# Four constants on SyncE's queue, and other planned times in the first sequence of a Flamingo kernel

## The chip, the cores and the metric

The kernel runs on one core of a Trainium2 chip. The metric is the time of one execution on the device, in microseconds (us). The kernel before was timed three times; its profile is of one further execution.

## The reference

Input `x` is 8 sequences of 256 tokens with 512 channels, `ctx` has the same shape. Two layers follow each other, each of an attention-like recurrence (`wkv`) and a feed-forward part, each added to `x` with a gate tanh(g):

```python
x = x + tanh(g_xattn[0]) * wkv0(layernorm(x), ctx)       # decay w, bonus u; a scan over 256 tokens
x = x + tanh(g_ffn[0])   * ffn0(layernorm(x))            # 512 -> 2048 -> 512
x = x + tanh(g_xattn[1]) * wkv1(layernorm(x), ctx)
x = x + tanh(g_ffn[1])   * moe1(layernorm(x))            # 8 experts, 2 for each token
# wkv: k = layernorm(x), v = ctx, one step of the scan for each token and channel
#   y_t = (e1 * p + e2 * v_t) / (e1 * q + e2);  p, q = running sums with decay w, kept stable by a running maximum o
# ffn0: hidden = silu(x W1^T) * (x W3^T); hidden = fwht(hidden) / sqrt(2048); out = hidden W2^T
# moe1: route by x gate^T, then silu(x w1) * (x w3), times w2, weighted by the route
```

`fwht` is a Walsh-Hadamard transform over the 2048 hidden units. The kernel applies it to W2 instead of to the hidden units: once with a 128 x 128 Hadamard matrix (`hadm`), once, after a turn of the rows through HBM, with a 16 x 16 one (`had16`).

## The kernel before, in words

Channels lie on partitions: a sequence's `x`, `ctx` and normed tiles are 128 partitions x 4 channel groups x 256 tokens, all in float32. Sequence 0 is taken in two halves of 128 tokens (b = 0, 1), so that TensorE gets its first large products earlier; sequences 1 to 7 are taken whole. In front of the loop over the sequences stand the loads and the first sequence:

- SyncE's queue loads x and ctx of sequence 0 by halves (`load_first`, L261 and L262), then W2 in 16 loads (L325) and W1 and W3 of the first feed-forward part in 16 (`fill_w13`, L279), then x of sequence 1 (`load_x`, L249). The transformed W2 is stored to `turned` (L631) and read back (`fill_w2`, L287) on the same queue.
- ScalarE's queue loads the constants with `load_const` (L301): `w0c`, `u0c`, `hadm`, `tgx` (gates of the recurrence), and then those that only later steps read: `w1c` and `u1c` (decay and bonus of layer 1), `tgf` (gates of the feed-forward parts) and `gate` (the router's weights). A DMA is started by an instruction in the engine's own stream, so what follows it on the engine waits for it.
- Each DMA waits, in the built program, for the landing of the DMA eight before it on the two queues together, as they share eight semaphores.

The steps that matter here, with their lines:

- `layernorm` (L434 to L473): VectorE adds the four channel groups (`s_k` or `s_f`, L434 and L436), TensorE takes the mean (`mean_k`, `mean_f`, L440), VectorE subtracts it (L442), ScalarE squares (`sq`, L446), VectorE adds (`q_k`, `q_f`, L450 and L452), TensorE takes the variance (`var`, L459), VectorE adds the epsilon (L464), GpSimd takes the power (L466), TensorE spreads it over the partitions (`rstd`, L471) and VectorE multiplies (L473). Names with `k` are norms ahead of a recurrence, names with `f` those ahead of a feed-forward part.
- `decayed_max`, the recurrence of layer 0, for each pair of channel groups: VectorE scans the running maximum (L545) and subtracts it (`dd`, L550), ScalarE makes the exponents (Relu, L557 and L559, then Exp, L562), VectorE adds the bonus to `dd` (L566) and multiplies by ctx (`ev`, L569), ScalarE takes `dd`'s Exp (L571), VectorE scans `q` (L574) and `p` (L576) and adds the denominator (L584). The three `carry` copies for the second half of the tokens are ScalarE's (L580). `attend` takes the reciprocal (L515), the products and the update of `x` (L509 to L521).
- `transform` (L623 and L625): one matmul of a 128 x 512 block of W2 with a Hadamard matrix into one of three PSUM banks `ps_o`, and ScalarE's copy back into the weights. A float32 matmul of the program is two MATMUL rows in the trace. `fwht_kj` is the first pass of 16 transforms and their stores, and runs as three lines in parallel; `fwht_i` is the second pass.
- `set_up` prepares the constants of later steps on ScalarE and VectorE (L391 to L412): `w1c` becomes the decay of layer 1, `tgf` gets its tanh, `had16` is made from `hadm`.
- `unit` (L798 to L809) is one hidden unit block of the feed-forward part: 8 matmuls into a PSUM bank `gl` (three banks), tanh on ScalarE (`t_f`, L805), two products on VectorE (L807, L809).

The order in which the instructions stand on TensorE, ScalarE, VectorE and GpSimd is not left to the compiler. While it is built, the kernel keeps a plan: each step is a `Line`, a generator that names an engine and a planned length before it writes its instructions (`pe`, `dve`, `act`, `pool`), and a line that is due at the earliest planned time is written next. `until` gives a step an earliest planned time; `near[0]` is the planned gap between two steps of one line on the same engine, `least[0]` the shortest planned matmul. For the first sequence (`alone(0, 1)`) the plan has its own values, and after it the ordinary ones. The planned times have no effect on the chip other than through this order: each engine works through its own stream in order and waits where a semaphore tells it to.

Behind the first sequence each sequence s runs its hidden units and its output on TensorE, with the recurrence of s + 1 (layer 0) and of s - 1 (layer 1) worked in beside it, and then the tokens are sent to the queues of their experts. Experts 6 and 7 are begun early, and the eight experts' products fill the rest of the time from about 770 us.

Of the kernel before, what the change touches and what calls it, by code (L numbers as in the profile page):

```python
# [17 lines left out]
P = 128  # L18
# [5 lines left out]
DC = D // P  # L24
# [5 lines left out]
NE = 8  # L30
# [20 lines left out]
def flamingo_kernel(  # L51
# [20 lines left out]
    nc = tc.nc  # L72
# [10 lines left out]
    def v4(name, shape=(P, DC, T)):  # L83
        return work.tile(list(shape), FP, tag="v4", name=name, bufs=35)
# [34 lines left out]
    lines = []  # L119
    LATER = 1e9  # L120
    near = [0.16]
    least = [0.28]
    SLACK = 0.8
    WAIT = 0.25
# [5 lines left out]
        return "V", 0.09 + 0.00105 * slope * width, False  # L130

    def act(width, slope=1.0):
        return "A", 0.2 + 0.0008 * slope * width, False

    POWER = ("G", 0.8, False)

# [7 lines left out]
    def until(time):  # L144
        return "T", time, False
# [54 lines left out]
    def joined(n, make):  # L200
        ends = []

        def told(at):
            ends.append(at)
            if len(ends) == n:
                make(max(ends))

        return told
# [14 lines left out]
    def alone(*levels):  # L223
        while any(line.level in levels for line in lines):
            start, i = min((line.starts(), i) for i, line in enumerate(lines))
            next(
                line for line in lines if line.op[0] == lines[i].op[0] and line.starts() <= start + WAIT
            ).write()
# [11 lines left out]
    queue = dram.tile([NE * NT, ROW], FP, name="queue")  # L240
# [6 lines left out]
    def load_x(s):  # L247
        x[s] = v4(f"x{s}")
        nc.sync.dma_start(out=x[s], in_=x_in[:, :, s * T : (s + 1) * T])  # L249
# [9 lines left out]
    def load_first(b):  # L259
        bs = slice(b * P, (b + 1) * P)  # L260
        nc.sync.dma_start(out=x[0][:, :, bs], in_=x_in[:, :, bs])  # L261
        nc.sync.dma_start(out=first_ctx[:, :, bs], in_=ctx_in[:, :, bs])  # L262
# [4 lines left out]
    def new_w13(name):  # L267
        return tuple(
            [[v4(f"{t}_{name}_{i}{j}", (P, 2, D)) for j in range(2)] for i in range(2)] for t in ("w1", "w3")
        )  # L270
# [4 lines left out]
    def fill_w13(tiles, *srcs):  # L275
        for j in range(2):
            for t, src in zip(tiles, srcs):
                for i in range(2):
                    nc.sync.dma_start(  # L279
                        out=t[i][j],  # L280
                        in_=src[i * 2 * P : (i + 1) * 2 * P, j * D : (j + 1) * D].rearrange("(c p) h -> p c h", p=P),
                    )
        return tiles
# [12 lines left out]
    def w2_of(w, k):  # L296
        return w[k // 2][:, k % 2, :]

    def load_const(src, shape, name):
        t = const.tile(shape, FP, tag=name, name=name)  # L300
        nc.scalar.dma_start(out=t, in_=src)  # L301
        return t

    load_first(0)
    w0c, u0c = load_const(w0, [P, DC], "w0c"), load_const(u0, [P, DC], "u0c")

    early = const.tile([P, 1], FP, tag="early", name="early")
    nc.vector.memset(early, 0.0)
    nc.scalar.activation(early, early, AF.Square)
    hadm = load_const(had, [P, P], "hadm")  # L310
    tgx = load_const(g_xattn.partition_broadcast(P), [P, 2], "tgx")
    load_first(1)
    wcol = [w0c, load_const(td1, [P, DC], "w1c")]
    ucol = [u0c, load_const(tf1, [P, DC], "u1c")]
    tgf = load_const(g_ffn.partition_broadcast(P), [P, 2], "tgf")
    gate = load_const(gateT, [P, DC, NE], "gate")

    w2h = [new_w2(n) for n in "ab"]
    turned = dram.tile([H0, D], FP, name="turned")
# [1 line left out]
    def by_kj(ap, i):  # L321
        return ap.rearrange("(k j i) d -> i k j d", j=8, i=16)[i]

    for i in range(16):
        nc.sync.dma_start(out=w2_of(w2h[i // KC], i % KC), in_=by_kj(W2T, i))  # L325
    w13 = [fill_w13(new_w13(n), *(w[:, i * HH : (i + 1) * HH] for w in (W1T, W3T))) for i, n in enumerate("ab")]
    load_x(1)


    def constant(shape, name, dt=FP):  # L330
# [13 lines left out]
        out=before, in_=ones, compare_op=ALU.is_gt, fill=0.0, base=0,  # L344
# [39 lines left out]
    def set_up_x():  # L384
        yield act(2)
        nc.scalar.activation(tgx, tgx, AF.Tanh)

    def set_up():

        yield act(4)  # L390
        nc.scalar.activation(wcol[1], wcol[1], AF.Exp)  # L391
        yield act(2)
        nc.scalar.activation(tgf, tgf, AF.Tanh)
        yield dve(4)
        nc.vector.tensor_scalar(wcol[1], wcol[1], -1.0, None, ALU.mult)

        yield act(4)
        nc.scalar.activation(decay, wcol[1], AF.Exp)
        yield dve(4)
        nc.vector.tensor_scalar(less, ucol[1], -1.0, 0.0, ALU.mult, ALU.min)  # L400
        yield dve(4)
        nc.vector.tensor_scalar(more_u, ucol[1], 0.0, None, ALU.min)
        yield dve(1)
        nc.vector.tensor_scalar(tgf_half, tgf[:, 1:2], 0.5, None, ALU.mult)
        yield dve(16)
        nc.vector.tensor_copy(token, token_i)


        yield dve(P)
        nc.vector.tensor_tensor(had16, hadm, hadm[:, 112:113].to_broadcast([P, P]), ALU.mult)  # L410
        for base, sign in ((0, 1), (15, -1)):
            nc.gpsimd.affine_select(  # L412
                out=had16, in_=had16, compare_op=ALU.is_ge, fill=0.0, base=base,
                pattern=[[-16 * sign, 8], [0, 16]], channel_multiplier=sign,
            )
# [75 lines left out]
    def first_norm(b):  # L491
        bs = slice(b * P, (b + 1) * P)
        yield from layernorm(x[0][:, :, bs], first_k[:, :, bs], f"k0_0_{b}")
# [125 lines left out]
    def transform(mat, i, scale):  # L619
        yield pe(D)  # L620
        w = w2_of(w2h[i // KC], i % KC)
        ps = ps_o.tile([P, D], FP, tag="o", name=f"fw_{i}")
        nc.tensor.matmul(ps, lhsT=mat, rhs=w, start=True, stop=True)  # L623
        yield act(D)
        nc.scalar.activation(w, ps, AF.Copy, scale=scale)  # L625

    def fwht_kj(j):
        for i in range(j, 16, 3):
            yield until(12.0 + 0.8 * i)
            yield from transform(hadm, i, 1.0)  # L630
            nc.sync.dma_start(out=by_kj(turned, i), in_=w2_of(w2h[i // KC], i % KC))  # L631

# [2 lines left out]
    def fwht_i():  # L635
        for h in range(2):
            latest_load[0] = fill_w2(w2h[h], turned[h * HH : (h + 1) * HH, :])
        return [chain(*(transform(had16, k, 0.5 / H0 ** 0.5) for k in range(j, 16, 2))) for j in range(2)]
# [713 lines left out]
    norm = [first_norm(b) for b in range(NB)]  # L1352
# [8 lines left out]
        mybir.EngineType.PE, mybir.EngineType.Activation, mybir.EngineType.DVE, mybir.EngineType.Pool  # L1361
    }
    with tc.manual_schedule(engines=ordered):
        near[0], least[0] = 0.08, 0.5

        finals = [
            joined(2, lambda at, b=b: Line(norm_f[b], level=2 * b, at=at)) for b in range(NB)
        ]
        second = [
            joined(2, lambda at, hf=hf: Line(half[1][hf], level=2, at=at, then=(finals[1],))) for hf in range(2)  # L1370
        ]

        def first_halves(at):
            for hf in range(2):
                Line(half[0][hf], level=0, at=at, then=(finals[0], second[hf]))

        Line(norm[0], level=0, at=3.7, then=(first_halves,))
        Line(norm[1], level=2, at=22.0, then=second)
        Line(set_up_x(), level=1, at=7.0)
        Line(set_up(), level=2, at=45.0)  # L1380
        turns = [Line(fwht_kj(j), level=1, at=0.0) for j in range(3)]
        alone(0, 1)
        near[0], least[0] = 0.16, 0.28
    fw = fwht_i()
    take(clear_queues())
    with tc.manual_schedule(engines=ordered):
# [182 lines left out]
```

## Time and profile before

| | us |
|---|---|
| timed runs (3): median | 1506.26 |
| timed runs: lowest, highest | 1505.01, 1506.66 |
| profiled execution: its own time | 1504.14 |
| profiled execution: span from first to last instruction | 1502.4 |
| TensorE busy in the span | 1460.9 (97%) |
| mean granted TensorE clock | 0.992 |

In the profile's rows a time is counted from the start of the span. A row of the timeline has start, duration, engine, line of the kernel, operation, output and inputs, shape and count; in brackets stands how long the engine was idle before it, and what ended that. `SPq` and `ACTq` are the sequencers of SyncE and ScalarE, where DMAs are issued. A row with a count merges instructions that follow each other. In the answers by stretches of time the count beside a busy time is that of the instructions, and the granted clock is a share of full speed; no clock is on record before 17 us, where 1.00 is printed.

### The profile page before, as it was taken

Reading aid. Unit: us, or ns where it says so; the run is one execution under the profiler, and the core shown is the slowest. Engines: PE = TensorE matmul, PEld = TensorE weight load, DVE = VectorE, ACT = ScalarE, POOL = GpSimd, SP = SyncE. Lnnn points to the kernel's source line nnn. Section 1 sums busy time; section 2 is a strip of 40 time slices with the busy share of each in tenths; the row PEclk is TensorE's granted clock in tenths of the full one; section 3 lists DMA queues with packets and bytes.
Section 4 is the critical chain, followed back from the end, with each engine's and each line's share of the span. In section 5 each row is a group of like instructions: output and inputs, shape, how many; then the busy total and the mean of one; then the engine's idle time right before and its main releaser. Section 6 shows DMA issues by size and latency. Waiting matters only on the chain. (4 is left out here: it accounts for less than half of the span.)

```text
span 1502.4 us, 19409 instructions
## 1 busy us (share of the span) xinstructions
PE 1460.9 (97%) x7336; PEld 1243.9 (83%) x7336; DVE 981.1 (65%) x2288; ACT 288.4 (19%) x677; POOL 245.2 (16%) x258
## 2 busy tenths in 40 slices
PE   6999999999999999999999999999999999999996
PEld 3888888888888888888877667688988889898894
DVE  5772886968788697876538413476647666476763
ACT  4340313213032321312111200011101111111110
POOL 1110111212122121312112200112301011010110
PEclk9999999999999999999999999999999999999998
DMA  9970001001100110115061314165124151330110
GB/s 324 355 264 14 12 31 43 28 36 37 41 29 29 50 35 15 43 30 182 15 248 38 97 36 161 35 199 201 60 86 153 40 205 43 108 137 28 60 33 18
DMA packets 79498, 135.16 MB, mean 90 GB/s; under 512 B 13084, under 2 KB 26524, under 8 KB 79392
## 3 DMA queue, kind: packets, MB, share of 16 engines
q1 hardware_dynamic: 69280, 108.45, 21.1%
q0 software_dynamic: 8960, 25.25, 4.8%
q8 instruction: 62, 1.02, 0.3%
q14 instruction: 44, 0.36, 0.1%
q10 hardware_dynamic: 1152, 0.09, 0.1%
HBM read 100.05 MB, written 37.90 MB: 92 GB/s over the span
## 5 line engine op out<-in xcount | busy, mean ns | idle before, releaser
L798 PE MATMUL gl_f<-xn,w_a 128*128 128x256 f32 (+1 forms) x1152 | 234.5, 359 | 1.0 <-DVE xn L473 1.0
L798 PE MATMUL gl_f<-xn,w_b 128*128 128x256 f32 (+1 forms) x1152 | 226.2, 357 | 0.0
L798 PEld LDWEIGHTS gl_f<-xn,w_a 128*128 128x128 f32 x1152 | 200.4, 192 | 27.9 <-issue 4.5
L798 PEld LDWEIGHTS gl_f<-xn,w_b 128*128 128x128 f32 x1152 | 200.5, 192 | 23.1
L781 PE MATMUL gl<-q,w_e 128*128 128x256 f32 x768 | 173.4, 384 | 6.0 <-DVEq L1479 4.0
L781 PEld LDWEIGHTS gl<-q,w_e 128*128 128x128 f32 x768 | 146.1, 193 | 26.6 <-issue 7.2
L969 POOL DMA_INDIRECT out<-g,who_e x40 | 46.3, 1158 | 502.3 <-DVE g L1231 407.0
L870 PE MATMUL o_f<-t_f,w_b 128*128 128x256 f32 x512 | 118.7, 380 | 0.0
L870 PE MATMUL o_f<-t_f,w_a 128*128 128x256 f32 x512 | 117.3, 380 | 0.0
L870 PEld LDWEIGHTS o_f<-t_f,w_b 128*128 128x128 f32 x512 | 96.2, 190 | 12.5
L870 PEld LDWEIGHTS o_f<-t_f,w_a 128*128 128x128 f32 x512 | 96.2, 190 | 12.5
L805 ACT ACTIVATE t_f<-gl_f 128x256 f32<-128x256 f32 (+1 forms) x144 | 50.0, 358 | 286.5 <-PE gl_f L798 286.0
L807 DVE SCALAR_TENSOR_TENSOR t_f<-t_f,gl_f 128x256 f32<-128x256 f32 (+1 forms) x144 | 53.6, 380 | 72.8 <-ACT t_f L805 72.4
L1156 PE MATMUL pa<-q,w_e 128*128 128x168 f32 x384 | 62.6, 306 | 0.0
L798 PE MATMUL gl<-q,w_e 128*128 128x256 f32 x256 | 58.4, 380 | 0.7 <-ACT q L920 0.7
L1156 PEld LDWEIGHTS pa<-q,w_e 128*128 128x128 f32 x384 | 57.4, 190 | 1.8 <-issue 1.3
L798 PEld LDWEIGHTS gl<-q,w_e 128*128 128x128 f32 x256 | 48.0, 190 | 11.1 <-issue 4.3
L1147 PE MATMUL y<-w_e,h 128*80 128x512 f32 (+1 forms) x128 | 56.9, 592 | 0.0
L785 ACT ACTIVATE t<-gl 128x256 f32<-128x256 f32 x48 | 18.4, 384 | 190.5 <-PE gl L781 190.5
L961 POOL DMA_INDIRECT g<-out,who_e x40 | 44.8, 1121 | 60.9 <-DMA out<-g,who_e 30.3
L515 DVE RECIPROCAL e<-e 128x512 f32<-128x512 f32 (+1 forms) x18 | 53.8, 2990 | 0.1
L809 DVE TENSOR_TENSOR t_f<-t_f,gl_f 128x256 f32<-128x256 f32 (+1 forms) x144 | 53.4, 379 | 0.7
(259 smaller groups left out, 2267.3 us busy)
## 6 DMA issues: line engine op xcount, KB each, us to landing
w_e<-in_w1T SPq DMA_DIRECT2D x32, 512.0 KB
w_e<-in_w3T SPq DMA_DIRECT2D x32, 512.0 KB
w_e<-in_w2T SPq DMA_DIRECT2D x32, 512.0 KB
queue<-empty SPq DMA_DIRECT2D x8, 1290.0 KB
r<-queue SPq DMA_DIRECT2D x32, 256.0 KB
c<-in_ctxT SPq DMA_DIRECT2D x15, 512.0 KB
out<-xr SPq DMA_DIRECT2D x16, 256.0 KB
x<-in_xT SPq DMA_DIRECT2D x7, 512.0 KB
```

Source lines behind the costliest of these rows:

```text
L515: nc.vector.reciprocal(den, den)
L781: nc.tensor.matmul(ps, lhsT=w13_of(w, c, k), rhs=xn(c)[:, :width], start=(c == 0), stop=(c == DC - 1))
L785: nc.scalar.activation(t, gp, AF.Tanh, scale=0.5)
L798: nc.tensor.matmul(ps, lhsT=w13_of(w, c, k), rhs=xn(c)[:, :width], start=(c == 0), stop=(c == DC - 1))
L805: nc.scalar.activation(t, gp, AF.Tanh, scale=0.5)
L807: nc.vector.scalar_tensor_tensor(t, t, 1.0, gp, ALU.add, ALU.mult)
L809: nc.vector.tensor_tensor(t, t, lp, ALU.mult)
L870: nc.tensor.matmul(o, lhsT=w2_of(w2h[k // KC], k % KC)[:, c * P : (c + 1) * P], rhs=hs[k], start=(k == 0), stop=(k == 2 * KC - 1),)
L961: nc.gpsimd.indirect_dma_start(out=g, out_offset=None, in_=out[:end, :], in_offset=bass.IndirectOffsetOnAxis(ap=who[:, b : b + 1], axis=0) ...
L969: nc.gpsimd.indirect_dma_start(out=out[:end, :], out_offset=bass.IndirectOffsetOnAxis(ap=who[:, b : b + 1], axis=0), in_=g, in_offset=None ...
L1147: nc.tensor.matmul(ys[b][:rows, :], lhsT=ts[k][:, b * P : b * P + rows], rhs=w2_of(w2, k), start=(k == 0), stop=(k == KC - 1),)
L1156: nc.tensor.matmul(ps[:, to, :], lhsT=weights[:, c, k * P : (k + 1) * P], rhs=toks[:, c, :], start=(c == 0), stop=(c == 1),)
```

## The change

Three things are changed, all in the first sequence or ahead of it.

1. `load_const` takes a queue, and `w1c`, `u1c`, `tgf` and `gate` are loaded from SyncE's queue, behind the W2, W1 and W3 loads and ahead of x of sequence 1. Before, they were issued from ScalarE's queue behind `tgx`.
2. In the plan of the first sequence the fixed part of a ScalarE step (`base[0]`) is 0.1 us instead of 0.2, the gap `near[0]` is 0.0 instead of 0.08, and the first norm is planned from 3.2 us instead of 3.7. After the first sequence both values are what they were.
3. The 16 transforms of the first pass over W2 are planned 0.86 us apart instead of 0.8.

```diff
+    base = [0.2]
...
     def act(width, slope=1.0):
-        return "A", 0.2 + 0.0008 * slope * width, False
+        return "A", base[0] + 0.0008 * slope * width, False
...
-    def load_const(src, shape, name):
+    def load_const(src, shape, name, queue=nc.scalar):
         t = const.tile(shape, FP, tag=name, name=name)
-        nc.scalar.dma_start(out=t, in_=src)
+        queue.dma_start(out=t, in_=src)
         return t
...
     load_first(1)
-    wcol = [w0c, load_const(td1, [P, DC], "w1c")]
-    ucol = [u0c, load_const(tf1, [P, DC], "u1c")]
-    tgf = load_const(g_ffn.partition_broadcast(P), [P, 2], "tgf")
-    gate = load_const(gateT, [P, DC, NE], "gate")
...
     w13 = [fill_w13(new_w13(n), *(w[:, i * HH : (i + 1) * HH] for w in (W1T, W3T))) for i, n in enumerate("ab")]
+
+    wcol = [w0c, load_const(td1, [P, DC], "w1c", nc.sync)]
+    ucol = [u0c, load_const(tf1, [P, DC], "u1c", nc.sync)]
+    tgf = load_const(g_ffn.partition_broadcast(P), [P, 2], "tgf", nc.sync)
+    gate = load_const(gateT, [P, DC, NE], "gate", nc.sync)
     load_x(1)
...
         for i in range(j, 16, 3):
-            yield until(12.0 + 0.8 * i)
+            yield until(12.0 + 0.86 * i)
             yield from transform(hadm, i, 1.0)
...
-        near[0], least[0] = 0.08, 0.5
+        near[0], least[0], base[0] = 0.0, 0.5, 0.1
...
-        Line(norm[0], level=0, at=3.7, then=(first_halves,))
+        Line(norm[0], level=0, at=3.2, then=(first_halves,))
...
         alone(0, 1)
-        near[0], least[0] = 0.16, 0.28
+        near[0], least[0], base[0] = 0.16, 0.28, 0.2
```

## The prediction

> **What bounds the kernel now.** I read the page first, then the granted clock by stretches, then the timeline of the first 72 us, engine by engine.
>
> ```profile
> PE 1460.9 (97%) x7336; PEld 1243.9 (83%) x7336; DVE 981.1 (65%) x2288; ACT 288.4 (19%) x677; POOL 245.2 (16%) x258
> PE   6999999999999999999999999999999999999996
> ```
> TensorE is busy 97% of the span; the only poor slice that this change can reach is the first (0 to 37.6 us).
>
> ```profile
> 34.20:37.50 3.30, 3.30 (x18) 3.30 (x17) 0.00 (x0) 0.00 (x0) 0.00 (x0) 0.50 1.05 387
> 37.60:61.40 23.80, 21.82 (x193) 21.58 (x192) 20.70 (x60) 8.56 (x33) 4.45 (x6) 1.00 0.95 344
> 61.50:64.80 3.30, 3.14 (x15) 2.87 (x15) 1.92 (x7) 0.63 (x1) 0.71 (x1) 0.50 1.01 364
> 64.90:72.00 7.10, 6.32 (x54) 5.91 (x53) 6.25 (x21) 2.48 (x8) 0.86 (x1) 1.00 1.04 377
> 72.00:140.00 68.00, 68.00 (x411) 57.45 (x410) 32.52 (x69) 18.66 (x43) 5.61 (x5) 1.00 0.49 171
> ```
> Columns: stretch, length, busy PE, PEld, DVE, ACT, POOL, then granted clock. From 72 us TensorE never rests; before that there are two half-clock spells, each behind a pause. So what counts is when TensorE starts the second half of sequence 0 (70.64 below): whatever it starts earlier, the end comes earlier.
>
> ```profile
> 7.56 0.49 ACTq L301 DMA_DIRECT2D gate<-in_gateT  x1
> 8.10 0.63 ACT L446 ACTIVATE sq_k<-k 128x512 f32<-128x512 f32 x1 [4.86 <-DMA w1c<-in_td]
> 11.34 5.33 PE L623 MATMUL fw<-w_a,hadm 128*128 128x512 f32 x6
> 17.98 1.56 ACT L625 ACTIVATE w_a<-fw 128x512 f32<-128x512 f32 x3
> 18.62 4.56 PE L623 MATMUL fw<-w_a,hadm 128*128 128x512 f32 x10 [1.95 <-DMA w_b<-in_W2T]
> 23.01 5.31 PE L623 MATMUL fw<-w_b,hadm 128*128 128x512 f32 x12
> 28.16 0.38 PE L440 MATMUL mean_f<-s_f,mean_m 128*128 128x128 f32 x2
> 33.41 4.57 PE L798 MATMUL gl_f<-xn,w_a 128*128 128x128 f32 x24 [0.22 <-DVE xn L473]
> 45.52 0.69 DVE L434 TENSOR_TENSOR s_k<-x 128x512 f32<-128x512 f32 x1 [0.66 <-DMA x<-in_xT]
> 50.62 1.19 DVE L442 TENSOR_TENSOR k<-x,mean_k 128x1024 f32<-128x1024 f32 x1
> 60.26 0.58 PE L459 MATMUL var_k<-mean_m,q_k 128*128 128x1 f32 x4 [1.98 <-DVE q_k L452]
> 65.11 1.22 DVE L473 TENSOR_TENSOR k<-k,rstd_k 128x1024 f32<-128x1024 f32 x1 [0.25 <-PE rstd_k L471]
> 70.64 1.16 PE L798 MATMUL gl_f<-xn,w_a 128*128 128x128 f32 x8 [0.78 <-DVE xn L473]
> ```
> ScalarE's first real step stands behind the issue of `gate`, though its input ended at 6.49. Three W2 transforms fill the three `ps_o` banks and TensorE waits 1.95 us for ScalarE to empty one. Then 22 matmuls in a row, one each 0.429 us (10 in 18.62 to 23.01), carry it to `mean_f`: the queue, not `s_f` (ready at 26.6), sets 28.16. Later TensorE waits 1.98 us in its own order for sequence 1's `var_k`, and pays a half-clock spell after it.
>
> **The four constants.** They leave ScalarE's queue: `sq_k` starts at 6.49 + 0.06 = 6.55, 1.55 us earlier; the chain to `dd` moves with it. On SyncE they stand behind all first weights and ahead of x of sequence 1 and the `turned` stores: four issues of 0.33 to 0.49 us (the L301 rows), about 1.5 us, hidden because that queue waits on landings there (`x` issued at 33.89, landed at 45.5). The waits in the built program tie each load to the landing of the one eight before it; four tiny loads take four of those places, so `x` is issued about 5 us later but still behind the same bytes. `x` is now first read near 48.8. `w1c` is first used by ScalarE near 46.1, and VectorE's negation stands behind that near 47.0, ahead of the scan, the denominator and the reciprocal. Its landing: lower bound 42 (the five weight tiles ahead at 1.35 us a tile, the pace at which L279's last loads are issued), upper 46.5 (11.6 us, as for `x`, from an issue near 35). I take 43: no cost.
>
> **The plan's figures.** The shorter step (0.1 for 0.2 us), the gap (0.0 for 0.08), the start 3.2 and the spacing 0.86 add no instruction: the built program has the same instructions on TensorE, VectorE, ScalarE and GpSimd, less the four issues; only their order in the first 140 us differs. On GpSimd the two selects of `had16` move behind one half's products (done near 53, used near 68): nothing.
>
> **The transforms.** In the built order one copy-out (L625) comes ahead of the three `carry` copies, and `dd`'s Exp (L571) after all four Relus. ScalarE's chain from 13.54 to 17.71 is back to back, so by its own steps the first copy-out starts at 16.04 (was 17.98) and TensorE resumes at 16.04 + 0.63 = 16.67 (was 18.62). But `dd`'s Exp loses 0.3 of its 1.55.
> Starting at 9.79, the first three transforms run at 0.853 a matmul until the clock rises, then 0.429: done near 14.3, so the pause is 2.4 us. In the trace a 3.41-us stretch less than about 30% busy (30.7 to 34.1, where `gl_f` fills the last 0.73; 58.0 to 61.4) was followed by half clock, one 55% busy (17.1 to 20.5) was not. If the stretches lie as before, 13.7 to 17.1 is 27% busy: I take half clock from 17.1 to 20.5, 5 matmuls done by then, 17 x 0.429 = 7.3 left: `mean_f` at 27.8 (-0.4) and not 26.1 (-2.1).
> [...]
>
> **The norms of sequence 0 and 1.** `mean_f` to first `gl_f` is an unbroken chain of 5.25 us (28.16 to 33.41): 33.04. Half clock again from 34.15; `rstd_k` after 24 matmuls at 37.16 (was 37.82), VectorE's k at 37.47 (was 38.13, -0.66). Then VectorE is the bound. Start to start from the rows:
> - Ahead of half 0's reciprocal (52.68) there go the wait for `x` 0.66, the second add of `s_k` 0.34, `had` 0.20, k's subtraction 1.12 and a scan 0.61: 2.93. 52.68 - 0.66 - 2.93 = 49.1; one wait for a `t_f` makes it 49.3.
> - To half 1's reciprocal (58.10, 5.42 later) come `had` 0.20, scan 0.61, add 0.34, and `q_k` 0.60 goes: 55.3.
> - To `s_f` (61.08, 2.98 later) comes k's 1.12, and 0.48 goes: 58.9. Its second add now stands behind `q_k`, which waits for ScalarE's `sq_k` (59.3), and four `t_f` steps: `mean_f` of half 1 at 61.1 (was 62.24).
> - TensorE reaches sequence 1's `mean_k` at 54.3, as `s_k` ends, and `var_k` directly behind `mean_f`: the 1.98 wait is replaced by 0.9 before `mean_f`, 70% or more of each stretch stays busy, so no half clock. 24 matmuls x 0.112: `var_f` 64.5 (was 67.58). VectorE's `q_f` no longer waits for k's 1.22. `rstd_f` 66.1, xn 66.5 behind k's product, first matmul of the second half at 67.26 (was 70.64): -3.4.
>
> After that I find no new pause: VectorE's sequence 1, half 0, is later by up to 6 us, because `t_f_0` now stands ahead of it, but the norm that it feeds is ready near 117 and is needed past 139. The PSUM banks of the second half come free 4 us or more ahead of need. All orders are equal from sequence 1's hidden layer on, and the work is the same.
> The sum: span 1502.4 - 3.4 = 1499.0; with the 1.74 around it, 1504.14 - 3.4 = 1500.7. The profiled execution lies 2.1 under the median 1506.26 of the timed runs (spread 1.65): by the same difference, 1502.9.
>
> **Rivals.**
> 1. Full clock. If the pause is not answered by half clock, `mean_f` is at 26.1 and `gl_f` at 31.4; with a half-clock spell there still, -5.2; if that spell alone goes, -4.7; with neither, -6.4. For it: the borderline share of 27 to 38% busy. Against: 27% was followed by half clock in the rows. About 1501.0 (1499.9 to 1501.6).
> [...]
> 2. Eaten. Another half-clock spell in the second half's norm (1.7 us), or the waits for `sq_k` and `t_f` grow so that `mean_f` stays at 62.2 (1.1 us): 1504.0 to 1505.7, say 1504.6. For it: two pauses of 0.9 us stay, and the timed runs of before may already be free of the spell at 61.5.
> 3. Slower: `w1c` lands late. ScalarE's Exp of it and VectorE's negation hold everything behind them one for one from 47.0. At 50.4 the gain is gone; at 53.4 the kernel is 3 us slower: 1509.3. For it: three queues' bytes lie ahead of it. Against: its upper bound 46.5.
>
> **The numbers.** Forecast 0.44, full clock 0.22, eaten 0.24, slower 0.10. A measurement of this kernel tells about 0.2%, 3.0 us. The forecast's own spread is +-0.9 (0.3 each for the Exp that moved, the pause at `mean_k` and the `t_f` waits), so two thirds of its 0.44 lie beyond 3.0: 0.29, and with all of full clock 0.50 (rounded); within: the rest of the forecast and eaten, 0.40; slower: 0.10. The range 1499.8 to 1505.7 holds the first three and leaves out the last.
>
> **What would show it.** `sq_k` near 6.55 with no DMA ahead; first copy-out near 16.0 and a clock of 0.5 from about 17.1; `mean_f` 27.8; no PE wait at `var_k`; second half from 67.3. Wrong, if VectorE waits for `w1c`, if the first matmul of half 1 is not before 69, or if TensorE rests between 72 and 140.

## The result, and the profile after

The changed kernel takes 1499.87 us (median of 6 runs, 1498.96 to 1501.13), the kernel before 1505.63 us in the same session (6 runs, 1503.73 to 1509.18). The ratio is 0.9957 with a 95% interval of 0.9942 to 0.9973: 5.8 us, 0.4% shorter. A second measurement gave 0.9961 (0.9946 to 0.9975). The forecast was 1502.9, so the sign was right and the size a good half of what came. The profiled execution says something else: its span went from 1502.4 to 1498.9 us, by 3.5, and its own time is 1500.7; forecast were 1499.0 and 1500.7. So the working of the first 72 us held, and the difference lies between the profiled execution and the runs.

From the page of the changed kernel, busy time and the busy tenths of TensorE:

```profile
PE 1460.3 (97%) x7336; PEld 1243.5 (83%) x7336; DVE 982.1 (66%) x2288; ACT 288.2 (19%) x677; POOL 242.6 (16%) x258
PE   6999999999999999999999999899999999999996
```

The busy time is that of before (1460.9): the span has lost pauses, not work. The stretches of the first 140 us (stretch, length, busy PE, PEld, DVE, ACT, POOL, granted clock, DMA share, GB/s):

```profile
13.50:16.80 3.30, 1.05 (x3) 0.22 (x2) 2.94 (x6) 3.30 (x14) 0.74 (x2) 1.00 1.02 355
16.90:20.30 3.40, 3.40 (x5) 1.32 (x4) 3.26 (x8) 1.64 (x4) 0.56 (x1) 0.50 1.05 386
34.00:37.30 3.30, 3.30 (x18) 3.30 (x17) 0.00 (x0) 0.00 (x0) 0.00 (x0) 0.50 1.05 387
61.50:64.80 3.30, 2.90 (x25) 2.90 (x26) 2.76 (x11) 0.70 (x2) 0.78 (x1) 1.00 0.98 348
72.00:140.00 68.00, 68.00 (x412) 58.12 (x411) 32.77 (x71) 18.87 (x44) 5.63 (x5) 1.00 0.49 171
```

A stretch in which TensorE was busy 1.05 of 3.30 us is followed by half clock at 16.9, as forecast; the half clock at 34 is there again; the one that before had at 61.5 is gone, and between 72 and 140 us TensorE never rests. Such a stretch at half clock is called a spell below. In the one at 34 TensorE starts a `gl_f` matmul each 0.21 us, behind it each 0.11, so that about half of a spell is lost where TensorE has work: 1.7 of 3.4 us, 3.4 of 6.8, an estimate from the two paces. Rows of the timeline:

```profile
6.49 0.63 ACT L448 ACTIVATE sq_k<-k 128x512 f32<-128x512 f32 x1 [3.26 <-DVE k L444]
9.73 4.60 PE L625 MATMUL fw<-w_a,hadm 128*128 128x512 f32 x6
15.96 0.57 ACT L627 ACTIVATE w_a<-fw 128x512 f32<-128x512 f32 x1
16.58 6.25 PE L625 MATMUL fw<-w_a,hadm 128*128 128x512 f32 x10 [2.25 <-ACT w_a L627]
27.82 0.39 PE L442 MATMUL mean_f<-s_f,mean_m 128*128 128x128 f32 x2
33.08 2.17 PE L800 MATMUL gl_f<-xn,w_a 128*128 128x128 f32 x12 [0.22 <-DVE xn L475]
49.30 0.73 DVE L408 CAST token<-token_i 128x16 f32<-128x16 int32 x1
49.95 1.74 DVE L517 RECIPROCAL e<-e 128x256 f32<-128x256 f32 x1
61.90 0.46 PE L442 MATMUL mean_f<-s_f,mean_m 128*128 128x128 f32 x2 [0.81 <-DVE s_f L438]
62.23 0.58 PE L461 MATMUL var_k<-mean_m,q_k 128*128 128x1 f32 x4
67.89 1.16 PE L800 MATMUL gl_f<-xn,w_a 128*128 128x128 f32 x8 [0.91 <-DVE xn L475]
```

`sq_k` waits for VectorE and for no DMA; ScalarE's first copy-out (L627) comes at 15.96 and releases TensorE at 16.58; `var_k` stands directly behind `mean_f` and waits for nothing. The second half of sequence 0 starts at 67.89 where it started at 70.64.

The profiles of all kernels can be cut at two places: the start of the second half (the first `gl_f` row behind `rstd_f`), and the pause ahead of the turn of the first expert's rows (`rt`, near 765 us). Between these two there is nothing to choose: 695.04 or 695.05 us in every kernel whose work there is the same.

| profile | second half starts | from there to the pause near 765 | from the pause to the end | span |
|---|---|---|---|---|
| before | 70.64 | 695.04 | 736.7 | 1502.4 |
| before, once more | 71.77 | 695.04 | 738.9 | 1505.7 |
| changed | 67.89 | 695.05 | 736.0 | 1498.9 |
| changed, once more | 66.29 | 695.05 | 738.3 | 1499.6 |
| new order, constants on ScalarE's queue | 68.80 | 695.04 | 738.6 | 1502.5 |
| old order, constants on SyncE's queue | 69.97 | 695.04 | 741.6 | 1506.6 |

The last stretch has the same instructions in the same order in all of them, and yet takes 736.0 to 741.6 us. The two profiles with 736.0 and 736.7 have no spell behind the pauses near 765 and 860 us, the three with 738.3 to 738.9 have one there, and the one with 741.6 has two of 6.8 us.

### The profile page after: what moved, and what is told of

The parts are those of the page before. It is cut to its first block, busy times and chain, and to the rows that moved or that the text cites. A ratio compares the mean times of both kernels' runs of the same rounds, so it can differ in the third digit from the quotient of the medians.

```text
span 1498.9 us, 19407 instructions
## 1 busy us (share of the span) xinstructions
PE 1460.3 (97%) x7336; PEld 1243.5 (83%) x7336; DVE 982.1 (66%) x2288; ACT 288.2 (19%) x677; POOL 242.6 (16%) x258
## 5 line engine op out<-in xcount | busy, mean ns | idle before, releaser
L511 POOL TENSOR_TENSOR dd<-dd,c 128x512 f32<-128x512 f32 (+1 forms) x18 | 21.5, 1196 | 207.7 <-issue 84.8
```

The source lines that it names most:

```text
L511: nc.gpsimd.tensor_tensor(num, own, vv, ALU.mult)
```

## The experiments

Two theories stood against each other on the excess over the profiles' 3.5 us. Either the runs of the two kernels meet different numbers of half-clock spells, or the difference is something else than the clock. An experiment with added work uses matmuls of the identity with itself whose result nobody reads, two rows of 0.11 us each.

### Both kernels once more

The edit: none, for either kernel.

> The kernel before, unchanged, for more of its runs. What is open: the profiles of the two kernels differ by 3.5 us in span, the medians of their runs by 5.8. Theory (order and clock spells): the order of the work saves 3.0 to 3.5 us in every run; what is left of the median's difference is half-clock spells of 3.41 us, each of which costs 1.7 us, that fall differently from run to run. Then the runs of this kernel lie in steps of about 1.7 us between 1503.7 and 1509.2, a run that is 1.7 us longer has a mean clock lower by 0.001, and this profile shows another set of spells or another place of the 3.41-us grid against the kernel than the first one. Rival (not the clock): the runs differ by other things, and the mean clock is the same in a run of 1504 and in one of 1509.

> The changed kernel, unchanged, for more of its runs. Theory (order and clock spells): the runs fall into two groups, near 1499.0 with a mean clock of 0.994 to 0.995 and near 1500.9 with 0.992, one half-clock spell of 1.7 us apart, and few above, since the pause of 1.98 us near 60 us is gone; the median against the kernel before is 0.996. Rival (not the clock): a spread as wide as that of the kernel before, 5 us, at one clock.

Measured: 1506.51 us (12 runs, 1503.38 to 1509.43) against 1499.34 us (7 runs, 1499.17 to 1501.46). The clock goes with the time. Over all 121 runs of the kernel before that came beside the experiments, the median is 1503.6 at a mean clock of 0.992 (24 runs), 1506.1 at 0.990 (17) and 1510.2 at 0.987 (17): 1.3 us for each 0.001 (1.7 was expected). 44 of the 121 are at 0.989 or less. The 13 runs of the changed kernel are at 0.992 to 0.995, in the two groups that were expected: seven take 1499.0 to 1499.3 us and six 1500.7 to 1501.5. The first median, 1499.87, comes of three runs from each group and lies where no run does. So the first theory holds: the kernel before pays spells in many runs that the changed kernel does not meet. The clock isn't all: at 0.992 the medians are 1503.6 (24 runs) and 1501.1 (5 runs), 2.4 us apart. Where one of the spells lies, from the stretches of the kernel before's second profile:

```profile
858.20:861.60 3.40, 1.65 (x13) 1.17 (x12) 1.84 (x6) 1.00 (x4) 1.00 (x1) 1.00 0.28 107
861.70:868.40 6.70, 6.63 (x26) 5.24 (x25) 4.30 (x12) 3.54 (x11) 3.79 (x6) 0.50 0.10 39
```

TensorE is busy 1.65 of 3.40 us while it waits for the rows that are turned near 860 us, and then works 6.7 us at half clock. The first profile of the same kernel has the same pauses there (1.46, 0.30 and 0.22 us) and no spell behind them.

### Each part alone

The first kernel has the new plan and the old queue, the second the new queue and the old plan:

```diff
 # new order, constants on ScalarE's queue: the changed kernel with
-    wcol = [w0c, load_const(td1, [P, DC], "w1c", nc.sync)]   # and three more, behind the weights
+    wcol = [w0c, load_const(td1, [P, DC], "w1c")]            # behind load_first(1), as before
 # old order, constants on SyncE's queue: the changed kernel with
-        near[0], least[0], base[0] = 0.0, 0.5, 0.1           # and at=3.2, 0.86
+        near[0], least[0], base[0] = 0.08, 0.5, 0.2          # and at=3.7, 0.8
```

> The changed kernel with w1c, u1c, tgf and gate loaded from ScalarE's queue behind tgx again, as in the kernel before; the plan and so the order on the engines is that of the changed kernel. Theory (both parts needed, the order worth more): ScalarE's first squares at 8.10 again, TensorE resumes the transforms near 18.1, mean_f near 28.9, and from there the new order: second half near 69, between the two kernels, -1.0 to -2.5 us against the kernel before. Rival (it is the constants): nothing gained without them, within 0.5 us of the kernel before. Other rival (the order alone): the whole gain, -3.4 in span.

> The kernel before with only the four loads moved to SyncE's queue; the plan's figures and so the order on the engines are those of the kernel before. Theory (both parts needed, the order worth more): squares at 6.55, first copy-out near 16.4, TensorE resumes near 17.0, mean_f near 27.9; behind it the old order of VectorE with its wait of TensorE for var_k near 60 (2 us): second half at 69.6 to 70.0, -0.7 to -1.0 us against the kernel before. Rival (it is the constants): -2.5 us or more, second half before 68.5.

Measured: the new order without the moved constants 1502.26 us, 0.9974 (0.9963 to 0.9984) of the kernel before; the moved constants without the new order 1506.26 us, 0.9995 (0.9980 to 1.0011). Rows of the timeline of the first:

```profile
7.68 0.63 ACT L448 ACTIVATE sq_k<-k 128x512 f32<-128x512 f32 x1 [4.46 <-DMA w1c<-in_td]
17.15 0.57 ACT L627 ACTIVATE w_a<-fw 128x512 f32<-128x512 f32 x1
68.80 1.16 PE L800 MATMUL gl_f<-xn,w_a 128*128 128x128 f32 x8 [0.91 <-DVE xn L475]
```

and of the second:

```profile
6.46 0.63 ACT L448 ACTIVATE sq_k<-k 128x512 f32<-128x512 f32 x1 [3.24 <-DVE k L444]
69.97 1.16 PE L800 MATMUL gl_f<-xn,w_a 128*128 128x128 f32 x8 [0.78 <-DVE xn L475]
```

The second half starts at 68.80 with the order alone and at 69.97 with the constants alone, both near what was expected (69; 69.6 to 70.0). These are single profiles. Seven with the first 72 us of the kernel before start there between 69.1 and 72.0, so the 69.97 isn't told apart from them. By the medians the order alone gains 3.3 us, more than the 1.0 to 2.5 expected; its clocks, 0.991 to 0.995, are nearly those of the changed kernel. The constants alone open ScalarE as they should, 1.6 us earlier at `sq_k`, and little of it reaches the second half, since VectorE's old order and TensorE's wait for `var_k` stand behind. In the runs even that is not seen: the best takes 1501.8, 1.1 less than the kernel before's best, but 7 of 12 are at a clock of 0.989 or less and take 1505 to 1509. Its profile, at 0.987, shows why, in its stretches near 765 and 860 us:

```profile
764.20:767.50 3.30, 1.69 (x12) 1.31 (x11) 2.35 (x12) 0.50 (x1) 0.30 (x2) 1.00 0.88 250
767.60:774.30 6.70, 6.03 (x16) 4.55 (x15) 0.16 (x1) 0.58 (x1) 0.00 (x0) 0.50 1.00 331
859.80:863.10 3.30, 1.48 (x13) 1.19 (x12) 1.74 (x5) 1.03 (x4) 1.00 (x1) 1.00 0.21 82
863.20:869.90 6.70, 6.59 (x25) 5.24 (x25) 4.21 (x12) 3.51 (x11) 3.89 (x6) 0.50 0.10 39
```

Two spells of 6.8 us at half clock, by the estimate above about 3.4 us lost in each. None of the 12 runs with the new order and the old queue is at 0.989 or less. With the old order such clocks are in 7 of 12 runs with the constants on SyncE's queue and in 44 of 121 with them on ScalarE's.

### The spacing of W2's transforms

```diff
-            yield until(12.0 + 0.86 * i)
+            yield until(12.0 + 0.8 * i)
```

> The changed kernel with the 16 transforms of W2 planned 0.8 us apart again; the constants on SyncE's queue and the plan's other figures stay. In the built order the last transform now stands behind var_f and not ahead of mean_k, and three others change places; VectorE's order has the same steps. Theory (the gain of the first 72 us comes from the four loads and the shorter ScalarE steps): the start of the second half stays at 66.1 to 68, median within 1.0 us of the changed kernel's. Rival (spreading the transforms is what opens ScalarE for the first copy-out): first copy-out later than 16.0, second half after 69, median 1501 or more.

Measured: 1501.20 us (7 runs), 0.9955 (0.9939 to 0.9971); the changed kernel has 0.9957. The first copy-out is at 15.92 and the second half starts at 66.24, within the changed kernel's 66.1 to 67.9. The spacing is not what opens ScalarE; the rival falls. Its profile (clock 0.990) has spells behind both later pauses, of 6.8 us at 764.4 and of 3.4 us at 860.0; neither profile of the changed kernel has one near 860.

### Filling the later pauses

```diff
+        if name in FILLED:                     # {"6_0_0": 10, "6_1_0": 8}
+            filler = ps_gl.tile([P, P], FP, tag="gl", name=f"filler_{name}")
+            for _ in range(FILLED[name]):
+                nc.tensor.matmul(filler, lhsT=ident, rhs=ident, start=True, stop=True)
         tp = ps_st.tile([P, DC, P], FP, tag="st", name=f"rt_{name}")
```

> The kernel before with matmuls of the identity with itself, whose result nobody reads, in two of TensorE's later pauses: 10 (1.1 us at full clock) ahead of the first turn of an early expert's rows near 767 us, where it waits 1.2 to 1.7 us, and 8 (0.9 us) ahead of the turn near 859 us, where it waits 1.46 us. Both pauses are in both kernels. Theory (what the medians differ by beyond the order is half-clock spells behind these two pauses): no run has a mean clock under 0.990, the runs lie from 1502.8 to 1505, the median is near 1503.4, 2.1 us under the kernel before. Rival (the spells of the first 72 us make the difference, or something else than the clock): the spread stays at 1503 to 1510 and the median at 1505.5.

> The changed kernel with the same matmuls in the same two pauses. Theory (half-clock spells behind the later pauses fall often in the kernel before and seldom here): it gains little, at most the 1.7 us of the spell near 765 us in the runs that have it; median 1499.1, 0.2 to 0.8 us under the changed kernel; against the kernel before with the same fill it is 4.0 to 4.4 us shorter, which is what the order of the first 72 us is worth. Rival (the order is worth only 3.4 us, as the profiles said): 3.4 between the two filled kernels.

Measured: 1507.66 us (12 runs) and 1503.99 us (12 runs). The times are off because each matmul is two rows, so that 4.0 us were added and not 2.0, and the 8 near 859 stand behind a pause of 1.39 us that stays, and not in it. But the clocks answer: no run of either kernel is at 0.989 or less, the mean clocks are 0.9920 and 0.9923, neither profile has a spell near 765 or 860, and the changed kernel is then 3.7 us shorter (1507.66 - 1503.99), where the unfilled ones differ by 5.8 and 6.2. That is nearer to the 3.5 us of the profiles than to the expected 4.0 to 4.4; with 12 runs each, spread over 2.6 and 4.8 us, the two aren't told apart. The spread of the kernel before stayed (1505.4 to 1510.2), which the clock alone doesn't explain.

### Moving the later pauses against the grid of the clock

The traces' records of the granted clock show a grid: in the first profile of the kernel before it changes at 34.15, 37.56, 61.45, 64.87, 976.22, 983.05 and 1491.64 us, in that of the changed kernel at 16.89, 20.30, 33.96, 37.37, 972.62, 979.45 and 1488.03, and within each all are whole multiples of 3.4133 us apart. From each profile the place of a pause is its start less the last grid point. For the pause near 860 us, over the 16 profiles in which it isn't filled: a spell followed at places 3.25, 3.30, 0.05, 0.14, 0.22, 0.25 and 0.41, and none at 0.70, 0.87, 1.00, 1.06, 1.10, 1.11, 1.28, 1.43 and 1.85. The spell lasted 3.4 us at 3.25, 3.30 and 0.05, and 6.8 us at the other four. By the estimate above nothing, 1.7 or 3.4 us are lost there, and in these 16 profiles the place tells which. The longest pause, 3.8 to 4.1 us near 973, goes by its place too, over all 18: a spell of 6.8 us where it begins 0.35 to 1.18 us behind a grid point (12), one of 3.4 us at 2.55 to 2.78 (5), none at 1.54 (1). To move the place, work was added in sequence 3, where TensorE never rests (n matmuls):

```diff
+        if name == "f3_5":
+            for _ in range(n):
+                nc.tensor.matmul(gp[:, :P], lhsT=ident, rhs=ident, start=True, stop=True)
         for ps, w in ((gp, w1), (lp, w3)):
```

The first two were sized at 0.112 us a matmul, half of what it takes:

> The changed kernel with 17 matmuls of the identity with itself, whose result nobody reads, ahead of one hidden unit of sequence 3, in a stretch where TensorE never rests: 1.90 us of work, and everything behind comes 1.90 us later against the 3.41-us grid of the clock. Theory (the place of the grid against the two later pauses decides, and the first 72 us set it: the pause near 764 us began 1.95 to 3.06 us behind a grid point in the changed kernel's profiles, 0.77 to 1.08 in those with the old order, and near 857 us a spell came where the pause began 0.25 us or less behind a grid point and none from 0.87 on): it costs more than its 1.90 us in a part of the runs, which have a mean clock of 0.988 to 0.991 and take 1503 to 1506; the median is above 1501.8. Rival (the place does not matter, each run draws it anew): 1.90 us in every run, median 1501.3, clocks of 0.992 to 0.995 as in the changed kernel.

> The kernel before with 14 such matmuls in the same place: 1.57 us of added work, which moves the later pauses from 0.8 to 1.1 us behind a grid point to 2.3 to 2.7. Theory (the place of the grid against the later pauses decides, and the first 72 us set it): the runs with a mean clock of 0.988 or less are gone, none is above 1507, and the median is not longer than the kernel before's 1505.5 although there is more work: 1504.4 to 1505.5. Rival (the place does not matter): 1.57 us more in every run, median 1507.1, and runs up to 1511.

> The changed kernel with 10 matmuls of the identity with itself, whose result nobody reads, ahead of one hidden unit of sequence 3, in a stretch where TensorE never rests. Each is two rows of 0.112 us, so 2.24 us of work (the 17 of the run before were 3.8 us, more than a whole 3.41-us grid step, and moved the pauses by only 0.4). Theory (the place of the clock's grid against the pause near 857 us decides; a spell came where it began 0.25 us or less behind a grid point, none from 0.87 to 1.43): the pause now begins between 0.1 ahead of a grid point and 0.3 behind it, so that half of the runs or more pay 3.4 us there: mean clock 0.990 or less in these, median over 1503, above the 1499.3 + 2.2 = 1501.6 of the work alone. Rival (each run draws the place anew, whatever the order): 2.24 us in every run, median 1501.6, no run below a clock of 0.991.

> The kernel before with 6 such matmuls in the same place, 1.34 us of work: the pause near 859 us, which began 0.25 and 0.87 us behind a grid point in the two profiles of this kernel, now begins 1.6 to 2.2 us behind one. Theory (the place decides): the runs with a mean clock of 0.988 or less are gone, none is above 1508, the median is 1504.5 to 1505.6 in spite of the added work. Rival (each run draws the place anew): 1.34 us in every run, median 1506.9, and runs up to 1512.

> The changed kernel with 5 of the unread matmuls in sequence 3, 1.12 us of work. Theory (the place of the clock's grid against the pauses of 764 and 857 us decides): the pause near 857 us begins about 2.2 to 2.6 us behind a grid point, where no spell follows it; the pause near 764 us more often has its spell of 1.7 to 3.4 us. No run at 0.989 or less; median 1500.7 to 1502.5. Rival (each run draws the place anew): the work alone, 1500.6, clocks as in the changed kernel.

> The changed kernel with 15 of the unread matmuls, 3.36 us of work, which is one step of the grid (3.41) but for 0.05. Theory (the place decides): the pauses lie against the grid as in the changed kernel, so it costs its 3.4 us and no more: median 1502.7 to 1503.3, no run at 0.989 or less; it is then shorter than the kernel with 10 of them, 1504.3, which has less work. Rival (it is the amount of added work, or chance, that brings the runs at 0.989): more such runs than the 5 of 12 with 10 matmuls, median 1505 or more.

> The kernel before with 10 of the unread matmuls, 2.24 us of work. In the profiles with the old order, shifts taken off, the pause near 767 us begins 0.77, 0.87, 1.08, 1.18 and 3.11 us behind a grid point. Theory (the place decides): with 2.24 more these are 3.0 to 3.4 and 1.9, the pause near 859 us begins past 2.4 and has no spell: at most 1 run in 6 at 0.988 or less, median 1506 to 1508. Rival (the old order has such runs wherever the grid lies): a third of the runs or more at 0.988 or less, median 1508 or more.

> The kernel before with 15 of the unread matmuls, 3.36 us of work, one step of the grid. Theory (the place decides): it costs 3.4 us, median 1509 to 1510, and the clocks are spread as in the kernel before, a quarter to two fifths of the runs at 0.988 or less. Rival (the amount of added work counts): another share of such runs, above a half or none.

Measured, with the added work as the profiles show it and the moved place modulo 3.41:

| kernel | matmuls | work, us | moved by | median, us | the kernel before beside it | runs at 0.989 or less |
|---|---|---|---|---|---|---|
| changed | 0 | 0 | 0 | 1499.87, 1499.34 | 1505.63, 1505.54 | 0 of 13 |
| changed | 5 | 1.11 | 1.1 | 1503.64 | 1505.15 | 2 of 12 |
| changed | 10 | 2.23 | 2.2 | 1504.34 | 1507.28 | 5 of 12 |
| changed | 15 | 3.36 | 3.4 | 1506.89 | 1505.15 | 1 of 12 |
| changed | 17 | 3.79 | 0.4 | 1505.07 | 1505.57 | 0 of 12 |
| before | 0 | 0 | 0 | 1505.15 to 1507.28 | | 44 of 121 |
| before | 6 | 1.34 | 1.3 | 1510.38 | 1507.28 | 9 of 12 |
| before | 10 | 2.24 | 2.2 | 1507.22 | 1505.15 | 0 of 12 |
| before | 14 | 3.13 | 3.1 | 1512.01 | 1505.57 | 8 of 9 |
| before | 15 | 3.35 | 3.4 | 1511.18 | 1505.15 | 4 of 12 |

The column of the clocks speaks for the place in part. A move by 2.2 us gives the changed kernel runs at 0.989 or less (5 of 12) and leaves the kernel before without any (0 of 12). A move by a whole step gives back shares near the unshifted ones (1 of 12, 4 of 12). The kernel before with 10 matmuls costs 2.1 us over the one beside it, with 6, at less work, 3.1. But the mean clock doesn't tell which pause a spell follows; only a profile does, and there is one of each kernel. From the stretches of the changed kernel with 10, the pause near 860 lying at 3.30 as planned, the spell that it didn't have:

```profile
860.50:863.80 3.30, 1.72 (x13) 1.34 (x14) 1.86 (x5) 1.36 (x5) 1.00 (x1) 1.00 0.21 79
863.90:867.20 3.30, 3.24 (x17) 2.72 (x16) 2.67 (x10) 2.01 (x8) 2.46 (x4) 0.50 0.17 68
```

The kernel before with 10, whose clocks came as expected, has a spell at this pause too, in a profile at 0.991. The pause was to lie past 2.4 and lies at 0.05:

```profile
859.40:862.70 3.30, 1.61 (x13) 1.20 (x12) 1.80 (x5) 1.19 (x4) 1.00 (x1) 1.00 0.21 79
862.80:866.10 3.30, 3.24 (x15) 2.72 (x16) 2.62 (x9) 2.21 (x8) 2.46 (x4) 0.50 0.12 45
```

So its 0 of 12 don't show that the spell near 860 is gone. Other expectations failed outright. The kernel before with 6 should have lost the runs at 0.989 or less and has them in 9 of 12. Its profile, at 0.989, has the pause near 860 at 1.28 and no spell there, as the theory has it; its clock is lowered by spells of 6.8 us at 17.7 and behind a longer pause near 766. The changed kernel with 5 and with 15 should have had no such run and has 2 and 1; with 5 the pause near 860 lies at 0.22, not at 2.2 to 2.6, and a spell follows. And the times don't follow: in all but one of the eight kernels the added work costs 0.8 to 4.4 us more than itself (for the changed kernel, against the 6.0 us that it lies under the kernel before), a whole step (15) too. One part is in the profiles: the pause near 765 us, 1.16 to 1.70 us in the eight profiles without fill or shift, is 1.0 to 3.2 us in the shifted ones. In the kernel before with 6:

```profile
759.83 0.98 POOL L761 DMA_INDIRECT queue<-row,pl  x1 [4.40 <-DMA queue<-row,pl]
769.45 1.97 PE L920 MATMUL rt<-ident,r 128*128 128x128 f32 x8 [3.21 <-DMA r<-queue]
```

GpSimd scatters four blocks of rows one after the other, each behind the landing of the last; this wait took 4.40 us where the three such waits took 2.2 to 3.0 in most profiles, and the rows that TensorE waits for came so much later. So in the shifted kernels the pause near 860 is moved by this as well as by the added work. Why shifted kernels have such a wait more often stays open.

### Keeping TensorE busy in its first pause

```diff
+        if mat is hadm and i == 3:
+            filler = ps_st.tile([P, P], FP, tag="st", name="filler")
+            for _ in range(8):
+                nc.tensor.matmul(filler, lhsT=ident, rhs=ident, start=True, stop=True)
```

> The changed kernel with 8 matmuls of the identity with itself (1.8 us at full clock, nobody reads the result) between the third and the fourth transform of W2, where TensorE waits 1.5 to 2.4 us for ScalarE's first copy-out near 16. Theory (the pause brings the half-clock spell from 17, which TensorE pays): no half clock from 17 to 20, the transforms end 1.6 us earlier, mean_f as s_f is ready near 27.05 instead of 27.8, second half 0.8 us or more earlier than the 66.1 to 67.9 of the changed kernel's profiles; median 1498.3 to 1499.3 if the later pauses cost the same. Rival (VectorE sets the start of the second half, and the spells of the first 72 us cost nothing): second half at 66.1 to 67.9 as before. Other rival: the matmuls run before the clock rises, at 0.45 us each, and hold the fourth transform up: second half later by up to 1.5 us.

Measured: 1500.24 us (6 runs), 0.9951 (0.9934 to 0.9968) of the kernel before, which is not told apart from the changed kernel's 0.9957. Rows of its timeline, and two stretches near 1018 us:

```profile
13.81 1.95 PE L627 MATMUL filler<-ident 128*128 128x128 f32 x16
16.54 1.98 PE L629 MATMUL fw<-w_a,hadm 128*128 128x512 f32 x4 [0.77 <-ACT w_a L631]
64.52 1.16 PE L804 MATMUL gl_f<-xn,w_a 128*128 128x128 f32 x8 [0.91 <-DVE xn L475]
```

```profile
1016.40:1019.70 3.30, 1.30 (x8) 0.83 (x6) 3.04 (x10) 0.00 (x0) 1.03 (x1) 1.00 0.22 38
1019.80:1023.10 3.30, 3.30 (x8) 2.64 (x9) 0.10 (x1) 0.00 (x0) 0.00 (x0) 0.50 0.96 351
```

The theory of the spells' price holds in the first 72 us: no half clock there at all, and the second half starts at 64.52, 1.8 us before the changed kernel's better profile and 3.4 before the other. The rest gives it back: 740.1 us from the pause near 765 to the end, against 736.0 and 738.3, with a spell behind that pause and one at 1019.8 that no other unfilled kernel but one shows. No version beats the changed kernel.

## Why the prediction was right and where it failed

By its own steps:

- *ScalarE's queue.* `sq_k` at 6.49 (forecast 6.55), first transform 9.73 (9.79), first copy-out 15.96 (16.04), TensorE back at 16.58 (16.67), clock up at 13.5 (13.7; the clock's record begins at 13.47 with 1.00, and the transforms' matmuls, started 0.85 us apart up to 13.15, go on with one 0.59 behind), half clock from 16.9 (17.1), `mean_f` 27.82 (27.8), first `gl_f` 33.08 (33.04). TensorE was busy about a third of that stretch, and half clock followed. The reading behind the doubt was wrong: the two stretches called less than about 30% busy, 30.7 to 34.1 and 58.0 to 61.4, were busy 1.79 and 1.43 of 3.41 us, 52 and 42%, and the 27% set against rival 1 is in no such stretch of that profile. Rival 1 (full clock) didn't come in this profile, but it came in part in three of the seven with the changed first 72 us: in two the spell near 34 is missing, in one that near 17, and their second half starts at 66.1 to 66.4, 4.3 to 4.5 us before 70.64 (the rival had 4.7 and 5.2). That the median lies at the edge of this rival's range is chance, since the rival carried over the same 2.1. A small slip: 10 matmuls in 18.62 to 23.01 are one each 0.439 us, not 0.429, which the next 12 have; that is 0.1 us here.
- *The constants on SyncE.* `w1c` was issued at 32.17 and landed 10.3 us later, at 42.5 (forecast 43); nobody waits for it. Rival 3 falls.
- *VectorE's chain.* The first reciprocal came at 49.95 (49.3) and from there everything is about 0.6 to 0.8 us behind the forecast: `mean_f` of half 1 at 61.90 (61.1), second half at 67.89 (67.26). Two terms were too small. `rstd_k` stands at 37.49 (37.16), and the cast of `token` took 0.73 us where it took 0.16 before. In the new order it runs beside GpSimd's product (48.96 to 50.00) and ends with it, at 50.03.
- *The wait for `var_k`* is gone, 0.81 us before `mean_f` stand in its place (0.9), and no half clock follows: as forecast. Rival 2 (eaten) didn't come.
- *The sum.* -2.75 at the second half in the pair of profiles, -3.5 in span; forecast -3.4. Taken over seven profiles with the first 72 us of each kernel (the shifted and filled ones share them), the second half starts at 70.62 on average in the old (69.1 to 72.0) and at 67.19 in the new (66.1 to 67.9): -3.4. That the mean hits the forecast is in part luck: four of the seven lie near 67.9, where the forecast's spells came, and three near 66.3, where one of them didn't.
- *The step that failed* is the one from the profiled execution to the median, "by the same difference, 1502.9", and under it the sentence that after the first 72 us "the work is the same". The work is; its clock is not. The 2.1 us by which the profile of before lay under the median were carried over to the changed kernel as if they were a constant. They go with the clock: that profile has no spell near 765 and 860, and many runs of the kernel before are at a lower clock than its 0.992. In the changed kernel the median lies 0.8 us under the profiled execution's 1500.7, which belongs to the upper of its two groups. So the term was 2.1 and measured -0.8, and these 2.9 us are the whole miss (1502.9 - 1499.9 = 3.0). The -0.8 is luck in part, as six runs fell three and three.

Why the changed kernel meets fewer spells is shown in part. That the place of the pause near 860 and the spell behind it go together is shown by 16 of 16 profiles; that moving the pause brings the spell, by the changed kernel with 10 matmuls alone. That the first 72 us set this place is argued: against the start of the span the grid lay at 0.01 and 1.46 us in the two profiles of before and at 3.24 and 0.51 in those of the changed kernel, but the pause near 765 us, with the shifts taken off, begins 0.71 to 1.15 us behind a grid point in five of seven profiles of the old order (1.92 and 3.11 in the others) and 1.46 to 3.06 in all seven of the new; in the profile with the spacing of 0.8 it is 0.28. The end of a spell is a grid point, as it is a change of the clock, and from the start of the second half to the pause near 765 there were 695.04 or 695.05 us of the same work, which would tie the later pauses to the grid. Fifteen profiles bear this out: where the last of these spells ends at 64 to 67 us (four, all of the old order), the pause near 765 begins 0.71 to 1.08 us behind a grid point; where it ends at 35 to 41 (five), 1.46 to 2.16; where it ends at 20 to 25 (six), 2.60 to 3.11 in four, and 0.28 and 1.15 in the others. Of the old order's seven, the three without the spell near 61 have 1.15, 1.92 and 3.11. So the wait for `var_k` (1.98 us), which ended 1.2 us ahead of that spell, may be what the kernel before pays for later; no run tests that by itself. The failed moves and the longer pauses of the shifted kernels stay open.

## What to carry to other kernels

In this case the pause near 860 us (1.46 us in the first profile of the kernel before, 1.45 in that of the changed kernel) was followed by no spell, by one of 3.4 us or by one of 6.8, in 16 of 16 profiles by its place on the clock's grid, and that place differed from profile to profile: compare the kernels by many runs with their mean clocks, and cut the profiles into stretches, before a gain of 0.2 to 0.4% is put down to the edit. Don't carry the difference between one profile and a median from one kernel to another; ask which spells make it and whether the change moves them. Here the edit itself is worth 3.4 us on average, and by single profiles and the medians the order is worth more of it than the freed queue.

## What was not expected of the hardware

- Half clock came also behind stretches that weren't idle. Of the grid's steps at full clock in all 18 profiles, each in which TensorE was busy less than 43% was followed by half clock (38 of 38), none above 61% was, and between the two 30 were and 36 weren't, so the busy share alone doesn't tell. In the stretches shown above it came behind 1.05 to 1.72 busy us of 3.30 or 3.40.
- The spells lasted one step (3.4 us) or two (6.8 us). They lasted two where TensorE was busy 55 to 82% of the first step, and in one place (near 862 us, the turns' matmuls) at 97 to 98%. Behind TensorE's last matmul half clock stayed to the end of the span: from 1491.64 to 1502.4 us in the profile of before, from 1488.03 to 1498.9 in the changed kernel's.
- The cast of 128 x 16 integers on VectorE took 0.16 us alone and 0.73 us beside a product on GpSimd, and in all ten profiles with the new order it ended 0.03 us behind that product.
- GpSimd's wait for the landing of a scatter on its queue, ahead of the pause near 765, was 2.2 to 3.0 us in 14 profiles; in the other four, all of shifted kernels, one of the three was 3.5 to 4.4.
